# One-run float32r operands and a 29-column pitch for the low products of a binary 3x3 convolution

## The chip, the cores and the metric

The kernel runs on one core of one Trainium2 chip. The metric is the device time of one execution in microseconds. The engines named below are TensorE (PE in the profile, with its weight loads as PEld), VectorE (DVE), ScalarE (ACT), GpSimd (POOL) and SyncE (SP, which issues DMAs).

## The reference, cut to what matters

Four layers follow each other on 16 images of 256 channels of 28 x 28. The change is in layer 1, whose first part is a 3x3 convolution of signs with clipped float32 weights:

```python
residual = prelu(x, a_alpha1)
z = hardsign(x + _pc(a_move))
bw = jnp.clip(a_w, -1.0, 1.0)
y = conv_general_dilated(z, bw, (1, 1), ((1, 1), (1, 1)))
y = prelu(bn(y, a_bn1), a_alpha2)
...
u = einsum('bchw,oc->bohw', z2, bw2)
```

z holds only signs (hardsign's value is sign(x)), so the products are sums of weights with signs. Layers 0 and 2 are other binary convolutions, and layer 3 is attention over the 784 positions.

## The kernel before

Everything is in one function, `forward`, with helpers inside it. It is emitted twice: once as used here (`careful` is false), and once as a fallback that runs only if a flag asks for it, and doesn't run here.

In layer 1 the convolution uses a transformation along the image's height that makes two output rows out of four sums. For each image b, `transform` (VectorE) forms four combinations u = 0..3 of the padded sign rows, each 14 rows (HR) of 30 columns (S + 2) for two halves k of the channels. It writes them in bfloat16 to `vs16`, in which columns 0 and 29 of each row are zero, being combinations of the pads. `widen` (ScalarE, and VectorE for one at the start) copies each to `vs` in float32r, in the same layout. `move_on` copies `vs16` by DMA to `one_on`, shifted by one element, so that the middle tap of the bfloat16 products starts at an even column.

The weights are split in two. w1[0] holds float16 high parts and w1[1] float32r low parts. One sum, for an image b, a half mo of the output channels and a unit u, is 12 products of 128x128 weights with 14 x 28 = 392 (HN) columns: part 0, the six high products (k = 0, 1 and taps c = 0, 1, 2, on `vs16`, with `one_on` for the tap c = 1 from image 1 on), then part 1, the six low products on `vs`. All accumulate into one bank of PSUM, which has 512 columns, and are written as one run of 392. There are 16 x 2 x 4 = 128 such sums, so 768 high and 768 low products, all recorded at line 782.

Two sums share a tile `cv` of two banks. Units 1 and 2 make a pair: `sum_pair_a` (line 813, ScalarE) takes one bank into a temporary t, `sum_pair_b` (line 823, VectorE) adds and subtracts the other bank to and from it, into `uvs`. Units 0 and 3 make the other pair: `rows_out` (line 834, VectorE) adds each of its banks to `uvs` and writes the even and odd rows of y. `conv_pairs` issues both high parts of a pair first and then both low parts, `conv_pair` one whole sum, and `conv_alone`, used for the last image, gives a sum its own tile.

`iteration(b)` writes the order of PE, ACT, DVE and SP out by hand. While TensorE convolves image b, the other engines prepare image b + 1 (`enter` at line 732, `sign1` at line 738, `residual_a` and `residual_b`, `transform`, `widen`) and finish images b - 1 and b - 2 (`prelu_y`, the gates with their small products at lines 685 and 877, `branch1`, the 1x1 convolution `conv1x1` at line 909 with float32r operands read as one run of 392, `unit_u`, `unit_b`, `branch2`, `squares2`). `last_iteration` does the same for image 15. GpSimd's queue in these stages holds stores to memory (n0d at line 660, x2d at line 937), a few memsets and, between layer 0 and layer 1, four operations of `mom.doubt` for the flag that is used in layer 3.

Other lines that are spoken of: 376 are the products of `sign_layer` in layers 0 and 2, which read float16 signs in 14 rows of 28 from pads with a pitch of 30. In layer 0 all three taps come from the pads; later the middle tap comes from a copy shifted by one element. Line 392 is their first eviction on ScalarE. Line 478 (`keep_busy`) are idle products of 512 columns that bridge stretches where TensorE has nothing to do.

Of the kernel before, what the change touches and what calls it, by code (L numbers as in the profile page):

```python
# [27 lines left out]
F32 = mybir.dt.float32  # L28
FR = mybir.dt.float32r
F16 = mybir.dt.float16  # L30
BF16 = mybir.dt.bfloat16
I16 = mybir.dt.int16
I32 = mybir.dt.int32
AF = mybir.ActivationFunctionType
ALU = mybir.AluOpType
# [4 lines left out]
P = 128  # L40
B = 16
S = 28
N = S * S
HN = N // 2
HR = S // 2
# [31 lines left out]
def conv_seq_kernel(tc: tile.TileContext, d: dict, out: bass.AP):  # L77
    again = forward(tc, d, out, False)
    with tc.If(again > 0):
        forward(tc, d, out, True)  # L80
# [3 lines left out]
def forward(ctx: ExitStack, tc: tile.TileContext, d: dict, out: bass.AP, careful: bool):  # L84
# [3 lines left out]
    nc = tc.nc  # L88
    V, A, T = nc.vector, nc.scalar, nc.tensor
# [40 lines left out]
    def vtile(name):  # L130
        return const.tile([P, 2], F32, name=name)
# [334 lines left out]
    with tc.tile_pool(name="ps_conv", bufs=3, space=PSUM) as psc, \  # L466
            tc.tile_pool(name="ps_sm", bufs=2, space=PSUM) as pss:

        def conv_ps():
            return psc.tile([P, 2, 512], F32, tag="cv", name="cv")  # L470
# [9 lines left out]
        with tc.tile_pool(name="ph1", bufs=1) as ph:  # L480
# [21 lines left out]
            def temp(tag):  # L502
                return ph.tile([P, HN if careful else N], F32, tag=tag, name=tag, bufs=2)
# [83 lines left out]
            c1, c2, c3, c4 = (c_bn[:, i, :] for i in range(4))  # L587
            cc, zb2 = vtile("cc"), vtile("zb2")
            ra1, ra2, rf2, us1, ns1 = (vtile(q) for q in ("ra1", "ra2", "rf2", "us1", "ns1"))
# [7 lines left out]
            moved, b3c = vtile("moved"), vtile("b3c")  # L597
# [92 lines left out]
                    rows = slice(32 * g, 32 * g + 32)  # L690
                    tt(b_1[rows], h, b_1[rows], ALU.add)

            vs = ph.tile([P, 2, 4, 2, HR, S + 2], FR, tag="vs", name="vs")
            vs16 = vs if careful else ph.tile([P, 2, 4, 2, HR, S + 2], BF16, name="vs16")
            one_on = None if careful else ph.tile([P, 4, 2, HR, S + 2], BF16, name="one_on")

            def room_sums():
# [23 lines left out]
            def full(tag, name, bufs):  # L721
                return ph.tile([P, N], F32, tag=tag, name=name, bufs=bufs)
# [35 lines left out]
            def widen(b, u, copy=A.copy):  # L758

                if not careful:  # L760
                    v, w = (
                        t[:, b % 2, u].rearrange("p k i c -> p (k i c)") for t in (vs, vs16)
                    )
                    copy(v, w)  # L764

            rx = {}

# [5 lines left out]
                x = xs[b][:, k, :]  # L773
                V.scalar_tensor_tensor(x, rx.pop(k), ra1[:, k:k + 1], x, ALU.mult, ALU.add)

            def conv(b, mo, u, ps, parts=range(2)):

                for part in parts:
                    w, v = w1[part], (vs16, vs)[part]
                    moved = part == 0 and b > 0 and not careful  # L780
                    for k, c in [(k, c) for cs in (((0, 2), (1,)) if moved else ((0, 1, 2),)) for k in range(2) for c in cs]:
                        T.matmul(  # L782
                            ps.rearrange("p (a b) -> p a b", b=S),
                            lhsT=w[:, k, c, u, mo * P:(mo + 1) * P],
                            rhs=one_on[:, u, k, :, 0:S] if moved and c == 1 else v[:, b % 2, u, k, :, c:c + S],
                            start=((part, k, c) == (0, 0, 0)),
                            stop=((part, k, c) == (1, 1, 2)),
                        )


            uvs = wpool.tile([P, 2, 2, HN], F32, tag="wa", name="uvs")
            ys, us = {}, {}
            pairs = {}

            def conv_pair(b, mo, i, u, parts=range(2)):
                if i == 0 and 0 in parts:
                    pairs[b, mo, u > 0 and u < 3] = conv_ps()
                conv(b, mo, u, pairs[b, mo, u > 0 and u < 3][:, i, :HN], parts)

            def conv_alone(b, mo, i, u, parts=range(2)):  # L800
                if 0 in parts:
                    alone[i] = conv_ps()
                conv(b, mo, u, alone[i][:, i, :HN], parts)

            def conv_pairs(b, mo, *us):

                for part in range(2):
                    for i, u in enumerate(us):
                        conv_pair(b, mo, i, u, (part,))

            def sum_pair_a(b, mo):
                t = temp("t1")[:, :HN]
                A.activation(
                    t, pairs[b, mo, True][:, 0, :HN], AF.Identity, bias=c1[:, mo:mo + 1], scale=us1[:, mo:mo + 1]
                )
                pairs[b, mo] = t

            def sum_pair_b(b, mo):

                ps, t = pairs.pop((b, mo, True)), pairs.pop((b, mo))  # L820
                uv = uvs[:, mo]
                for i, s in enumerate((us1, ns1)):
                    V.scalar_tensor_tensor(uv[:, i], ps[:, 1, :HN], s[:, mo:mo + 1], t, ALU.mult, ALU.add)
                pairs[b, mo] = uv

            alone = {}

            def rows_out(b, mo, rows=range(2)):
                ps, uv = alone[rows[0]] if alone else pairs[b, mo, False], pairs[b, mo]
                if 0 in rows:  # L830
                    ys[b, mo] = full("yu", f"y{b}_{mo}", 6)
                two = ys[b, mo].rearrange("p (a two b) -> p two a b", two=2, b=S)
                for i in rows:
                    V.scalar_tensor_tensor(
                        two[:, i], ps[:, i, :HN].rearrange("p (a b) -> p a b", b=S), us1[:, mo:mo + 1],
                        uv[:, i].rearrange("p (a b) -> p a b", b=S), ALU.mult, ALU.add,
                    )

# [113 lines left out]
            def iteration(b):  # L952
# [15 lines left out]
                if two:  # L968
                    unit_b(b - 2, 0)
                    unit_b(b - 2, 1)  # L970
                sum_pair_a(b, 0)
                conv_pair(b, 0, 0, 0)
                h = hidden_a(b, hidden_x(b)) if one else None
                residual_a(b + 1, 0)
                sign1(b + 1, 1)
                sum_pair_b(b, 0)
                if one:
                    h = hidden_b(b, h)
                residual_a(b + 1, 1)
                residual_b(b + 1, 0)  # L980
                transform(b + 1, 1)
                residual_b(b + 1, 1)
                conv_pair(b, 0, 1, 3)
                rows_out(b, 0)
                if one:
                    g = gates(h)
# [3 lines left out]
                if one:  # L990
                    for k in range(2):
                        branch1_a(b - 1, k, g[:, 0])
                widen(b + 1, 1)
                conv_pairs(b, 1, 1, 2)
                for u in (1, 2):
# [9 lines left out]
                if two:  # L1005
                    branch2(b - 2, 0, g[:, 1])
                sum_pair_a(b, 1)
                sum_pair_b(b, 1)
                if one:
                    branch1_c(b - 1, 1)  # L1010
                widen(b + 1, 2)
                if two:
                    branch2(b - 2, 1, g[:, 1])
# [5 lines left out]
                for u in (0, 3):  # L1019
                    transform(b + 1, u)  # L1020
                    widen(b + 1, u)
# [3 lines left out]
                for s in aside[b + 1]:  # L1025
                    s.load()
                rows_out(b, 1)
                for late in lates:
                    late()
# [3 lines left out]
            def last_iteration(b):  # L1033
# [6 lines left out]
                for k in range(2):  # L1040
                    unit_b(b - 2, k)
                sum_pair_a(b, 0)
                h = hidden_b(b, hidden_a(b, hidden_x(b)))
                conv_pair(b, 0, 0, 0)
                sum_pair_b(b, 0)
                g = gates(h)
                for k in range(2):
# [3 lines left out]
                for k in range(2):  # L1051
                    branch1_b(b - 1, k)
                    branch1_c(b - 1, k)
                conv_pair(b, 1, 0, 1)
                rows_out(b, 0)
                squares2(b - 2, 0)
                branch2(b - 2, 1, g[:, 1])
# [7 lines left out]
                squares2(b - 2, 1)  # L1065
                px = hidden_x(B, TWO)
                conv_alone(b, 1, 0, 0, (0,))
                h = hidden_a(B, px, TWO)
                sum_pair_b(b, 1)
                h = hidden_b(B, h, TWO)  # L1070
                conv_alone(b, 1, 0, 0, (1,))
                rows_out(b, 1, (0,))
                g = gates(h, some=TWO)
                conv_alone(b, 1, 1, 3)
                branch2(b - 1, 0, g[:, 1])
                squares2(b - 1, 0)
# [13 lines left out]
            with tc.manual_schedule(engines={ET.PE, ET.DVE, ET.Activation, ET.SP}):  # L1090
# [23 lines left out]
                b = B - 1  # L1114
# [794 lines left out]
```

## Time and profile before

| | |
|---|---|
| time, median of 3 runs | 951.56 us (951.31 to 951.74) |
| profiled execution | 951.89 us |
| its span | 950.0 us |
| busy share PE, DVE, ACT, POOL | 98%, 80%, 71%, 14% |
| layer 1, its convolution | from 113.5 to 444.4 us |
| products at line 782, busy | 768 low 170.4 us, 768 high 168.6 us |
| granted TensorE clock, mean | 0.996 |

A line of a group names the code line, the engine and operation, out<-in by the program's names, for a product the weights' rows*columns and the moving operand's partitions x columns and type, and the count; then busy time and the mean duration of one, and the idle time of the engine before them with what ended it. Products overlap in the array, so a product's duration is longer than its share of the engine's time; the distance between the starts of two products is that share. The chain of waits is followed back from the last instruction to what released each, and is then shown in order of time: start, length, engine and line, number of instructions. A float32r operand is shown as f32 when a product reads it.

### The profile page before, as it was taken

To read this page: it belongs to the slowest core of one execution; us is meant where nothing else is said; L and a number is where in the kernel's file an instruction comes from. 1 tells how busy PE (TensorE), PEld (TensorE's weight loads), DVE (VectorE), ACT (ScalarE), POOL (GpSimd) and SP (SyncE) were. 2 spreads that over 40 slices of the span, in tenths; PEclk is the share of its full clock that TensorE was granted. 3 is DMA by queue.
4 is the path that set the end of the run, shared out by engine and by line. 5 is a ranking of instruction groups with operands and counts; after the bars stand their busy time and mean duration, and the time that the engine had idled before them with its cause. 6 is when DMAs were issued, how large, how long until landed. Compare 5 with 4: busy or idle time off the path is not lost.

```text
span 950.0 us, 14937 instructions
## 1 busy us (share of the span) xinstructions
PE 932.5 (98%) x5608; PEld 581.7 (61%) x5608; DVE 758.2 (80%) x1436; ACT 672.5 (71%) x1165; POOL 136.4 (14%) x145
## 2 busy tenths in 40 slices
PE   8999999999999999999999999999999999999995
PEld 4555678887888888787555555555444444444442
DVE  4777798999998899987788878889657767686865
ACT  6665568888887888865777757774867666666652
POOL 2001100000000000000000000000244343535340
PEclk9999999999999999999999999999999999999998
DMA  9877434445533444411655201111232524344212
GB/s 347 315 275 267 160 121 139 174 177 200 187 139 138 156 161 160 162 71 68 228 206 211 113 20 62 77 78 59 35 68 69 132 72 103 102 91 114 68 69 106
DMA packets 39334, 130.71 MB, mean 138 GB/s; under 512 B 4866, under 2 KB 16324, under 8 KB 39252
## 3 DMA queue, kind: packets, MB, share of 16 engines
q1 hardware_dynamic: 33332, 98.31, 28.9%
q0 software_dynamic: 5632, 30.54, 11.8%
q8 instruction: 46, 0.75, 0.3%
q10 hardware_dynamic: 288, 0.80, 0.2%
q14 instruction: 36, 0.29, 0.1%
HBM read 72.67 MB, written 32.11 MB: 110 GB/s over the span
## 4 chain that ended last, share of the span: by engine, by line
PE 95%; DVE 1%; ACT 1%; DMA 1%; SPq 1%; issue 0%; DVEq 0%; ACTq 0%
PE cv L376 30%; PE cv L782 29%; PE sc L1475 8%; PE av L1496 8%; PE cv L909 5%; PE mi L1452 5%; PE sm L1538 2%; PE unused L478 2%; PE mi L1556 2%; PE sm L1496 1%; DMA xs<-in_x_dram 1%; PE gate L877 1%; PE hid L685 1%; SPq L269 0%; DVE r L1522 0%
## 5 line engine op out<-in xcount | busy, mean ns | idle before, releaser
L782 PE MATMUL cv<-vs,w 128*128 128x392 f32 (+1 forms) x1296 | 272.4, 352 | 0.3 <-DVE vs L134 0.3
L376 PE MATMUL cv<-fpads,wpk 128*128 128x392 f16 (+1 forms) x1434 | 247.6, 329 | 1.7 <-DVE wpk L301 1.3
L376 PEld LDWEIGHTS <-wpk 128*128 128x128 f16 x1746 | 169.0, 97 | 124.4 <-DVE wpk L301 2.1
L782 PEld LDWEIGHTS cv<-vs,w 128*128 128x128 f32 x768 | 143.2, 190 | 6.3
L1479 ACT ACTIVATE es<-sc 128x784 f32<-128x784 f32 x112 | 87.3, 822 | 41.7 <-PE sc L1475 41.7
L782 PEld LDWEIGHTS <-w 128*128 128x128 f16 x768 | 69.4, 99 | 51.9 <-issue 9.1
L1475 PE MATMUL sc<-q,keyswa 64*128 64x392 f32 x448 | 89.9, 513 | 0.9 <-ACT es L1479 0.9
L1496 PE MATMUL av<-es,v 128*64 128x392 f32 x448 | 80.7, 499 | 0.0
L1239 DVE SCALAR_TENSOR_TENSOR p<-ab,vec 128x392 f32<-128x392 int16 x128 | 77.3, 617 | 0.0
L392 ACT ACTIVATE ab<-cv 128x392 int16<-128x392 f32 x64 | 31.8, 496 | 57.4 <-PE cv L376 54.5
L1489 POOL TENSOR_TENSOR sum<-sum,es 128x784 f32<-128x784 f32 x32 | 67.2, 2100 | 3.1 <-ACT es L1479 0.6
L1475 PEld LDWEIGHTS sc<-q,keyswa 64*128 64x128 f32 x448 | 38.9, 186 | 44.0 <-issue 17.1
L376 PE MATMUL cv<-shifted,wpk 128*128 128x392 f16 x312 | 60.2, 328 | 0.0
L782 PE MATMUL cv<-one_on,w 128*128 128x392 bf16 x240 | 59.4, 329 | 0.0
L1463 DVE COPY keyswa<-mi 64x392 f32<-64x392 f32 x31 | 16.3, 565 | 53.4 <-ACT q L1459 53.4
L1496 PEld LDWEIGHTS av<-es,v 128*64 128x64 f32 x448 | 29.4, 136 | 47.4 <-issue 47.0
L937 POOL DMA_DIRECT2D x2d<-x x16 | 8.6, 537 | 345.3 <-DVE x L931 284.9
L394 DVE SCALAR_TENSOR_TENSOR ab<-ab,cv 128x392 int16<-128x392 int16 x64 | 35.7, 558 | 27.7 <-ACT ab L392 27.5
L764 ACT CAST vs<-vs 128x840 fp32r<-128x840 bf16 x63 | 54.1, 882 | 2.5 <-DVE vs L134 2.5
L909 PE MATMUL cv<-z,fw 128*128 128x392 f32 x256 | 48.9, 342 | 0.1
L909 PEld LDWEIGHTS cv<-z,fw 128*128 128x128 f32 x256 | 46.1, 188 | 0.9 <-ACT z L901 0.9
L1452 PE MATMUL mi<-p,wqk 128*128 128x392 f32 x124 | 45.1, 505 | 0.1
(313 smaller groups left out, 1529.0 us busy)
## 6 DMA issues: line engine op xcount, KB each, us to landing
xs<-in_x_dram SPq DMA_DIRECT2D x30, 784.0 KB, 5.1
one_on<-vs SPq DMA_DIRECT2D x60, 209.8 KB, 2.7
x2d<-x POOLq DMA_DIRECT2D x16, 784.0 KB, 3.6
out_dram<-p SPq DMA_DIRECT2D x15, 784.0 KB, 3.8
shifted<-fpads SPq DMA_DIRECT2D x26, 449.8 KB, 2.7
p<-x2d POOLq DMA_DIRECT2D x14, 784.0 KB, 6.9
p<-x2d SPq DMA_DIRECT2D x13, 784.0 KB, 5.9
n0d<-n POOLq DMA_DIRECT2D x16, 392.0 KB, 4.4
```

Source lines behind the costliest of these rows:

```text
L376: T.matmul(pss[j][:, n // size if careful else h, :rows * S].rearrange("p (a b) -> p a b", b=S), lhsT=w[:, n, c, :], rhs=src[:, blocks[j][ ...
L392: A.activation(by_halves(ab[:, 1], blocks[j]), ps, AF.Copy, scale=1.0 / PACK)
L394: V.scalar_tensor_tensor(a, b, -PACK, ps, ALU.mult, ALU.add)
L764: copy(v, w)
L782: T.matmul(ps.rearrange("p (a b) -> p a b", b=S), lhsT=w[:, k, c, u, mo * P:(mo + 1) * P], rhs=one_on[:, u, k, :, 0:S] if moved and c == 1 ...
L909: T.matmul(ps[:, h, :HN], lhsT=w[:, k, mo * P:(mo + 1) * P], rhs=z2[b][:, k, h * HN:(h + 1) * HN], start=(k + i == 0), stop=(k + i == 2),)
L1239: V.scalar_tensor_tensor(p, y, alpha[:, mo:mo + 1], y, ALU.mult, ALU.max, accum_out=mom.sums[:, 0, at // 2:at // 2 + 1] if mom.by_sums(at, ...
L1452: T.matmul(ps[:, h, :HN], lhsT=wqk[:, k, :], rhs=x[b][:, k, h * HN:(h + 1) * HN], start=(k == 0), stop=(k == 1))
L1475: T.matmul(ps[:, h, :HN], lhsT=chunk[rows], rhs=qs[b][rows], start=True, stop=True)
L1479: A.activation(e, ps[:, :, :HN], AF.Exp, scale=0.125)
L1489: (V if late else nc.gpsimd).tensor_tensor(sums[b, late], sums[b, late], e, ALU.add)
L1496: T.matmul(ps[64 * h:64 * h + 64, :HN], lhsT=w, rhs=e[:, h, :], start=start, stop=stop)
```

## The change

The float32r tile `vs` drops one of the two zero columns: its rows are 29 apart instead of 30, so that the zero at the end of a row is the zero at the start of the next. A tap c of a low product then is the run of LONG = 14 x 29 = 406 elements that starts at c; each 29th column of the result is of no use. Two zeros are added behind the last row, by one memset on GpSimd. The sums in PSUM get the same pitch of 29: the low products write runs of 406, the high ones write 28 of every 29 columns, except for the first of each sum, which writes all 29 (reading 29 columns of each row), so that the 29th columns hold a number. `sum_pair_a`, `sum_pair_b` and `rows_out` read 28 of 29 through `of_rows`. `widen` copies 29 of 30 columns of each row. `vs16`, `one_on` and the weights stay as they are.

```diff
-            vs = ph.tile([P, 2, 4, 2, HR, S + 2], FR, tag="vs", name="vs")
-            vs16 = vs if careful else ph.tile([P, 2, 4, 2, HR, S + 2], BF16, name="vs16")
+            LONG = HR * (S + 1)
+            if careful:
+                vs = vs16 = ph.tile([P, 2, 4, 2, HR, S + 2], FR, tag="vs", name="vs")
+            else:
+                vs16 = ph.tile([P, 2, 4, 2, HR, S + 2], BF16, name="vs16")
+
+                vs = ph.tile([P, 2, 4, 2, LONG + 2], FR, tag="vs", name="vs")
+                nc.gpsimd.memset(vs[:, :, :, :, LONG:].bitcast(F32), 0.0)
+
+            def of_rows(ps, i, whole=False):
+
+                if careful:
+                    return ps[:, i, :HN].rearrange("p (a b) -> p a b", b=S)
+                return ps[:, i, :LONG].rearrange("p (a b) -> p a b", b=S + 1)[:, :, 0:S + whole]
...
             def widen(b, u, copy=A.copy):
 
                 if not careful:
-                    v, w = (
-                        t[:, b % 2, u].rearrange("p k i c -> p (k i c)") for t in (vs, vs16)
-                    )
-                    copy(v, w)
+                    v = vs[:, b % 2, u, :, 0:LONG].rearrange("p k (i c) -> p k i c", c=S + 1)
+                    copy(v, vs16[:, b % 2, u, :, :, 0:S + 1])
...
-            def conv(b, mo, u, ps, parts=range(2)):
+            def conv(b, mo, u, i, ps, parts=range(2)):
 
                 for part in parts:
                     w, v = w1[part], (vs16, vs)[part]
+                    long = part == 1 and not careful
                     moved = part == 0 and b > 0 and not careful
                     for k, c in [(k, c) for cs in (((0, 2), (1,)) if moved else ((0, 1, 2),)) for k in range(2) for c in cs]:
+                        if long:
+                            rhs = v[:, b % 2, u, k, c:c + LONG]
+                        elif not careful and (part, k, c) == (0, 0, 0):
+                            rhs = v[:, b % 2, u, k, :, 0:S + 1]
+                        else:
+                            rhs = one_on[:, u, k, :, 0:S] if moved and c == 1 else v[:, b % 2, u, k, :, c:c + S]
                         T.matmul(
-                            ps.rearrange("p (a b) -> p a b", b=S),
-                            lhsT=w[:, k, c, u, mo * P:(mo + 1) * P],
-                            rhs=one_on[:, u, k, :, 0:S] if moved and c == 1 else v[:, b % 2, u, k, :, c:c + S],
+                            ps[:, i, :LONG] if long else of_rows(ps, i, (part, k, c) == (0, 0, 0)),
+                            lhsT=w[:, k, c, u, mo * P:(mo + 1) * P], rhs=rhs,
                             start=((part, k, c) == (0, 0, 0)),
                             stop=((part, k, c) == (1, 1, 2)),
                         )
...
                 A.activation(
-                    t, pairs[b, mo, True][:, 0, :HN], AF.Identity, bias=c1[:, mo:mo + 1], scale=us1[:, mo:mo + 1]
+                    t.rearrange("p (a b) -> p a b", b=S), of_rows(pairs[b, mo, True], 0), AF.Identity,
+                    bias=c1[:, mo:mo + 1], scale=us1[:, mo:mo + 1],
                 )
...
-                uv = uvs[:, mo]
+                uv, ps1 = uvs[:, mo], of_rows(ps, 1)
                 for i, s in enumerate((us1, ns1)):
-                    V.scalar_tensor_tensor(uv[:, i], ps[:, 1, :HN], s[:, mo:mo + 1], t, ALU.mult, ALU.add)
+                    V.scalar_tensor_tensor(
+                        uv[:, i].rearrange("p (a b) -> p a b", b=S), ps1,
+                        s[:, mo:mo + 1], t.rearrange("p (a b) -> p a b", b=S), ALU.mult, ALU.add,
+                    )
...
                     V.scalar_tensor_tensor(
-                        two[:, i], ps[:, i, :HN].rearrange("p (a b) -> p a b", b=S), us1[:, mo:mo + 1],
+                        two[:, i], of_rows(ps, i), us1[:, mo:mo + 1],
                         uv[:, i].rearrange("p (a b) -> p a b", b=S), ALU.mult, ALU.add,
                     )
```

More of the change, by code (lines that the diff above doesn't have):

```diff
@@ L797, in conv_pair @@
                     pairs[b, mo, u > 0 and u < 3] = conv_ps()
-                conv(b, mo, u, pairs[b, mo, u > 0 and u < 3][:, i, :HN], parts)
+                conv(b, mo, u, i, pairs[b, mo, u > 0 and u < 3], parts)
             def conv_alone(b, mo, i, u, parts=range(2)):
@@ L802, in conv_alone @@
                     alone[i] = conv_ps()
-                conv(b, mo, u, alone[i][:, i, :HN], parts)
+                conv(b, mo, u, i, alone[i], parts)
             def conv_pairs(b, mo, *us):
```

## The prediction

> **What bounds the kernel now.** I read the chain of waits first, in order of time, because it says which engine's work is never waited out by another. From 114 us to 444 us, all of layer 1's 3x3 convolution, it is TensorE without a break. One image's pieces (start us, us, what):
>
> ```profile
> 235.75 6.43 PE cv L782 x36
> 242.19 0.32 PE hid L685 x4
> 242.51 2.25 PE cv L782 x12
> 244.76 0.34 PE gate L877 x4
> 245.10 8.56 PE cv L782 x48
> 253.66 2.88 PE cv L909 x16
> ```
>
> They add to 20.8 us per image, 96 of the 112 large products being the convolution's. The table by stages says whether another engine is near; the columns are window: us, then busy us of PE, weight loads, DVE, ACT, POOL, then the granted clock, the DMA share and GB/s:
>
> ```profile
> 235.00:256.00 21.00, 21.00 (x123) 17.17 (x122) 19.11 (x40) 18.54 (x30) 0.53 (x1) 1.00 0.50 182
> ```
>
> PE is busy all 21.0 us at full clock, DVE 19.1, ACT 18.5. So a nanosecond on a product of line 782 is a nanosecond on the end, and DVE and ACT have about 1.9 and 2.5 us per image in which to lose some. The groups by shape then give the two kinds of product (busy us, mean ns of one):
>
> ```profile
> L782 PE MATMUL cv<-vs,w 128*128 128x392 f32 x768 | 170.4, 367 | 0.0
> L782 PE MATMUL cv<-vs,w 128*128 128x392 bf16 x528 | 109.2, 330 | 0.3 <-DVE vs L134 0.3
> L782 PE MATMUL cv<-one_on,w 128*128 128x392 bf16 x240 | 59.4, 329 | 0.0
> L909 PE MATMUL cv<-z,fw 128*128 128x392 f32 x256 | 48.9, 342 | 0.1
> ```
>
> These durations overlap, since a product starts before the last one's results are out. What counts is the distance between starts, which the timeline of PE gives:
>
> ```profile
> 249.90 0.49 PE L782 MATMUL cv<-one_on,w 128*128 128x392 bf16 x2
> 250.24 0.83 PE L782 MATMUL cv<-vs,w 128*128 128x392 bf16 x4
> 250.90 0.49 PE L782 MATMUL cv<-one_on,w 128*128 128x392 bf16 x2
> 251.09 2.57 PE L782 MATMUL cv<-vs,w 128*128 128x392 f32 x12
> ```
>
> High products: 250.24 to 250.90 for four, 165 ns each. Low products: the two one_on products from 250.90 take 0.33, so the twelve low ones start in truth at 251.23, and the conv1x1 product after them starts at 253.50 by the same view: 2.27 / 12 = 189 ns; I use 189.5 (the x36 and x48 pieces, less their high half at 165.9, give 191 to 192 with the switches between kinds). The conv1x1 of line 909 has the same 128x128 float32 weight load and the same 392 columns, but reads them as one run: 2.88 / 16 = 180 ns (179.8). Rows therefore cost the low products 9.7 ns each, and that is what the change goes after.
>
> **The change, part by part.**
>
> *Low products, 768 of them.* Afterwards each reads one run, but of 406 columns. The price of a column: the 512-column products of line 478 lie on the chain as 6.47 us for 30, 215.7 ns; the fp16 products of line 376 as 38.99 us for 235, 165.9 ns for 392; (215.7 - 165.9) / 120 = 0.415 ns. Fourteen columns are 5.8 ns, so 179.8 + 5.8 = 185.6 ns, a gain of 3.9 each, 768 x 3.9 = 3.0 us. More than half of the rows' 9.7 ns goes to the added columns. Bounds: if the 180 ns of line 909 are set by the weight load (188 ns records, one per product) and not by the columns, 406 also cost 179.8 and the gain is 9.7 x 768 = 7.4 us; if the rows are not what costs, they take 189.5 + 5.8 = 195.3, a loss of 4.5 us. I take 185.6: clean column price, nearest row.
>
> *The first high product of each sum, 128 of them* (16 images x 2 halves of channels x 4 units), widens from 392 to 406 columns so that the 29th ones are written too: 128 x 5.8 = 0.74 us lost.
>
> *The other 640 high products* still have 392 columns, but write rows of 28 with a pitch of 29 into PSUM, where all large products of this trace write one run. This is the open price. Below: nothing, if the writing side takes any address; a gain is excluded, since 392 columns at 0.415 are already all of their 165 ns but 3. Above, the nearest row is a reader's: line 376 in layer 0 reads all three taps from the pads, so every third product's 14 rows begin one 2-byte element off, and its chain piece is 35.18 us for 207, 170.0 ns against the 165.9 of the later stage where a shifted copy serves that tap. Three times 4.1 is 12.2 ns for 14 rows on an odd element, 0.87 a row. With pitch 29, every second output row starts on an odd element: 7 x 0.87 = 6.1 ns if the writer pays as the reader does, 640 x 6.1 = 3.9 us. If all 14 rows pay, 12.2 ns, 7.8 us. I take 6.1, as odd starts are what that row shows paying, and even starts (taps 0 and 2 there) pay next to nothing. The break-even is (3.0 - 0.74) / 640 = 3.5 ns per product.
>
> [...]
>
> *The reads of PSUM with pitch 29* (ACT line 813, DVE lines 823 and 834). Line 834 already uses rows (618 ns), line 823 one run (616 to 622): rows as such cost nothing on DVE. ACT's 662 ns may grow; nothing shows it. Even 10% on all of them is 2 x 4 x 0.06 = 0.5 us per image, spread over the two engines and covered by their 1.9 and 2.5 us. Uncovered it would be 0.5 x 16 = 8 us, but PE would have to run into their results, and the waits view has no product of layer 1 waiting longer than 0.3 us.
>
> *Widening* copies 812 instead of 840 elements: 63 ACT casts of 881 ns, at 0.83 ns an element ((822 - 496) / 392, line 392) 23 ns less each; nothing for the end, as PE does not wait for them. The one DVE cast at 114.72 (597 ns) may fall to DVE's slower rate of 1.05 ns ((1030 - 618) / 392), 0.3 us more; it would end at 115.6, and unit 2's low products come six products after 115.81. Cover 1.3 us; without it 0.3 us.
>
> *The POOL memset* stands behind the last n0d store (108.56 us, waiting for DVE) and ahead of four operations for doubts that nobody needs before layer 3. A 128x1 memset there took 0.10 us; this one of 32 elements may take 0.3. It adds a wait of PE for POOL; behind it are all products of layer 1, but the first that reads the zeros starts at 115.81, six us later. No DMA is added or moved; move_on still copies from the bf16 tile.
>
> **Sum.** -3.0 + 0.74 + 3.9 = +1.6 us. The profiled execution took 951.89 (span 950.0 and 1.9 around it) and would become 953.5; the median shown is 0.33 lower, so 953.2. That is +0.17%, inside the 0.2% that a measurement can tell from no change.
>
> **Rivals.**
>
> 1. *Pitched writes are free.* For: high products here read rows of 28 with a pitch of 30 at 165 ns, next to the bare column price. Against: odd rows on the reading side are not free. -3.0 + 0.74 = -2.3: 949.3.
> 2. *Every row of a pitched write pays*, the mechanism that ends slower: TensorE's write of 14 separate rows, at 12.2 ns on each of 640 products. It decides from about 6.5 ns on, where the sum reaches +1.9 us. For: float32 rows at even and odd starts alike cost the low products about 10 ns on the reading side, and sums are float32. Against: 2-byte rows at even starts pay nothing. -3.0 + 0.74 + 7.8 = +5.5: 957.1.
> 3. *The low products gain nothing* (the rows are not their cost; the change then doesn't do what it is said to): 195.3 ns each, +4.5 + 0.74 + 0 to 3.9: 956.8 to 960.7. Against: line 909, alike in all but the rows.
> 4. *Weight loads set the 180 ns*: -7.4 + 0.74 + 0 to 3.9: 944.9 to 948.8. For: each float32 load is recorded with 188 ns. Against: the loads of line 877, before products of 2 columns, follow each other faster than that (four products in 0.34 us on the chain).
>
> **Chances.** Forecast 0.36, rivals 0.30, 0.22, 0.06, 0.06. Faster by over 0.2% (under 949.7): most of rival 1 (0.24) and rival 4, 0.30. Within: the rest of rival 1 and two thirds of the forecast, 0.06 + 0.24 = 0.30. Slower (over 953.5): the forecast's upper third 0.12, rivals 2 and 3, 0.40. The range runs from 948.6, below rival 1, to 958.5, above rival 2: it leaves out rival 4, most of rival 3 and the tails of 1 and 2, under 0.2. The forecast's own range, from a write price of 4 to 8 ns, is 951.9 to 954.4.
>
> **What would show it.** Low group, now 128x406: mean 367 down by about 4, and the distance between starts near 185.6; 180 speaks for rival 4, 195 for rival 3. High group of 392 columns: mean 330 up by 6; unchanged is rival 1, up by 12 rival 2. The first high product: up by 6, or, if pitch costs, less than the others. The chain must still be TensorE throughout; if ACT or DVE appear in it between 120 and 440 us, the covered costs were not covered. An x48 piece (24 low, 4 first and 20 other high products) would go from 8.56 to 8.61 us by the forecast (-0.094 + 0.023 + 0.122), to 8.49 by rival 1, to 8.73 by rival 2.

## The result and the profile after

The changed kernel takes 953.86 us (median of 15 runs, 952.38 to 955.29), the kernel before, on the same chip, 951.9. The ratio is 1.002 with a 95% interval of 1.0013 to 1.0027: slower by about 1.9 us, on the edge of what was to be called no change. The forecast was +1.6 us. The profiled execution took 954.27 us, its span is 952.2.

The chain of waits after, in order of time, answers the pieces shown of before (start us, us, what; the products moved from line 782 to 799):

```profile
236.34 6.50 PE cv L799 x36
242.84 0.32 PE hid L685 x4
243.17 2.26 PE cv L799 x12
245.43 0.34 PE gate L897 x4
245.77 8.61 PE cv L799 x48
254.38 2.87 PE cv L929 x16
```

It is still TensorE throughout, and each piece with convolution products is a little longer: x36 6.43 to 6.50, x48 8.56 to 8.61 as forecast. The sharpest measure is the time per image, from the start of one 1x1 convolution to that twelve images later. Before (line 909) and after (line 929):

```profile
170.50 2.88 PE cv L909 x16
...
419.98 2.88 PE cv L909 x16
```

```profile
170.75 2.87 PE cv L929 x16
...
421.63 2.87 PE cv L929 x16
```

That is 249.48 / 12 = 20.790 us before and 250.88 / 12 = 20.907 after: 0.117 us an image, 1.9 us for 16, all of the loss. The groups by shape after (busy us, mean ns) show its parts:

```profile
L799 PE MATMUL cv<-vs,w 128*128 128x406 f32 x768 | 167.9, 363 | 0.0
L799 PE MATMUL cv<-vs,w 128*128 128x392 bf16 x400 | 89.8, 337 | 0.3 <-DVE vs L134 0.3
L799 PE MATMUL cv<-one_on,w 128*128 128x392 bf16 x240 | 61.1, 338 | 0.0
L799 PE MATMUL cv<-vs,w 128*128 128x406 bf16 x128 | 44.4, 347 | 0.0
```

The low products got shorter although they have 14 columns more (367 to 363). The high ones of 392 columns, whose operands did not change, got longer (330 and 329 to 337 and 338); what changed for them is the write into rows with a pitch of 29, and the experiments test that. The 128 first ones are the longest of the high ones. The other engines' work is as it was: the three readers of pitched sums take 667, 622 and 616, and 618 ns, as before (666, 622 and 616, 618), and the casts 860 instead of 882.

### The profile page after: what moved, and what is told of

It reads as the page before. It is cut to its first block, busy times and chain, and to the rows that moved or that the text cites. A ratio compares the mean times of both kernels' runs of the same rounds, so it can differ in the third digit from the quotient of the medians.

```text
span 952.2 us, 14947 instructions
## 1 busy us (share of the span) xinstructions
PE 933.3 (98%) x5602; PEld 581.3 (61%) x5608; DVE 758.3 (80%) x1436; ACT 671.6 (71%) x1165; POOL 136.3 (14%) x146
## 4 chain that ended last, share of the span: by engine, by line
PE 95%; ACT 1%; DMA 1%; DVE 1%; SPq 1%; issue 0%; DVEq 0%; ACTq 0%
PE cv L376 30%; PE cv L799 29%; PE sc L1495 9%; PE av L1516 8%; PE cv L929 5%; PE mi L1472 5%; PE sm L1558 2%; PE unused L478 2%; PE mi L1576 2%; PE sm L1516 1%; DMA xs<-in_x_dram 1%; PE gate L897 1%; PE hid L685 1%; ACT es L1499 0%; SPq L269 0%
## 5 line engine op out<-in xcount | busy, mean ns | idle before, releaser
L799 PE MATMUL cv<-vs,w 128*128 128x406 f32 (+2 forms) x1296 | 273.7, 353 | 0.3 <-DVE vs L134 0.3
L774 ACT CAST vs<-vs 128x812 fp32r<-128x812 bf16 x63 | 52.6, 860 | 2.4 <-DVE vs L134 2.4
```

Source lines behind the costliest of these rows:

```text
L774: copy(v, vs16[:, b % 2, u, :, :, 0:S + 1])
L799: T.matmul(ps[:, i, :LONG] if long else of_rows(ps, i, (part, k, c) == (0, 0, 0)), lhsT=w[:, k, c, u, mo * P:(mo + 1) * P], rhs=rhs, start ...
```

## Experiments

Two theories of the pitched write were to be told apart. Theory 1: a row of PSUM that starts on an odd element costs TensorE extra, an even one nothing. Theory 2 (the forecast's rival 2): every separate row costs. All images' times below are worked out as above, over the same twelve images.

**One run for the high products.** The edit to the changed kernel, in `conv`:

```diff
-    ps[:, i, :LONG] if long else of_rows(ps, i, (part, k, c) == (0, 0, 0)),
+    ps[:, i, :LONG] if long else of_rows(ps, i, True) if not careful and (part, k, c) == (0, 0, 0)
+    else of_rows(ps, i) if careful else img(ps[:, i, 0:0 + HN]),
```

> The changed kernel, but with 640 high products (all but the first of each sum) writing their 392 columns as one run, as in the kernel before; the low products still read and write runs of 406. High and low sums then do not lie on the same columns, so the output is not the reference's: it is a kernel for its time only. Theory 1 (rows written from an odd start pay) and theory 2 (every row of a pitched write pays) agree: the distance between the starts of those high products returns from 171.5 to 165 ns, 4.0 us of the changed kernel's 953.9 go, and what is left is the low products' gain less the widened first ones: 949.5 to 950.3. If the price lay elsewhere (evictions reading with a pitch, widening, the memset), the time stays near 953.9.

Measured: 951.48 us beside 952.26 of the kernel before, a ratio of 0.9992 (0.9983 to 1.0001). Behind another high product, these products return to the 165 ns from start to start that they had before. The chain of this kernel:

```profile
170.47 2.87 PE cv L930 x16
...
419.15 2.87 PE cv L930 x16
```

20.723 us an image, 0.184 below the changed kernel. Forty such products an image: the write with pitch 29 costs 4.6 ns each. What the change wins without it, 0.067 us an image or 1.1 us in all, is less than the 1.6 to 2.4 expected; the first high products explain most of that (below).

**Pitch 30, even and odd.** In both, the first high product writes 420 columns, so that every later write lies on written columns, and the others write 28 of 30 from column 0, or from column 1:

```diff
+    def rows30(ps, i, at, n):
+        return ps[:, i, :HR * 30].rearrange("p (a b) -> p a b", b=30)[:, :, at:at + n]
...
-    rhs = v[:, b % 2, u, k, :, 0:S + 1]
+    rhs = v[:, b % 2, u, k]
...
-    ps[:, i, :LONG] if long else of_rows(ps, i, (part, k, c) == (0, 0, 0)),
+    ps[:, i, :LONG] if long else of_rows(ps, i) if careful
+    else rows30(ps, i, 0, S + 2) if (part, k, c) == (0, 0, 0) else rows30(ps, i, 0, S),
```

> The changed kernel, but with the 640 high products writing rows of 28 with a pitch of 30, so that every row starts on an even element, and the first high product of each sum writing all 30 columns of each row (420). High and low sums do not lie on the same columns, so the output is not the reference's. Theory 1 (odd starts pay): high products at 165 to 166 ns apart, time as with one run plus 0.7 us for the wider first product: 950.3 to 951.0. Theory 2 (every row pays): 171.5 ns, 954 to 955.

> As the kernel with a pitch of 30, but each of the 640 high products' rows starts one element later, so that all 14 rows start on an odd element. The output is not the reference's. Theory 1: twice the price of pitch 29, which has 7 such rows: 165 + 12.5 = 177 to 178 ns apart, 958 to 959.5. Theory 2: 171.5 ns, 954 to 955.

Measured: 951.36 (0.9991, 0.9982 to 1.0) for even rows and 957.55 (1.0055, 1.0041 to 1.0069) for odd ones. The chains and one group of each, even first:

```profile
170.73 2.87 PE cv L933 x16
...
419.41 2.87 PE cv L933 x16
```

```profile
L802 PE MATMUL cv<-one_on,w 128*128 128x392 bf16 x240 | 59.5, 329 | 0.0
```

```profile
171.85 2.87 PE cv L933 x16
...
425.65 2.87 PE cv L933 x16
```

```profile
L802 PE MATMUL cv<-one_on,w 128*128 128x392 bf16 x240 | 62.6, 344 | 0.0
```

Even: 248.68 / 12 = 20.723 us, the same as one run. Odd: 253.80 / 12 = 21.150 us, 0.427 more, 10.7 ns for each of the 40 products. The two programs differ only in the column on which the rows start. Seven odd rows cost 4.6 ns, fourteen 10.7, fourteen even ones nothing: theory 1 holds and theory 2 falls. Fourteen odd rows were expected to cost 12.5 ns; the mean is less, for a reason given below. All rows have 28 columns, so one that starts on an odd column also ends just before one (columns 1 to 28, the next is 29), and the runs can't say which of the two ends is paid for. That the first product's 420 columns cost no more than its 406 in rows of 29 (20.723 us both) is taken up below.

**One run from column 1.** As the first experiment, with `ps[:, i, 1:1 + HN]`.

> The changed kernel, but with the 640 high products writing one run of 392 that starts on column 1. The output is not the reference's. Theory 1, in its form that an odd row costs one access more: one access of 0.9 ns per product, so 166 ns apart, 0.6 us above the run that starts on column 0, about 950.5. If instead every pair of an odd run were split, the products would take far more than 171.5 ns and the time would pass 960. Theory 2: no price, as the run starting on column 0.

Measured: 951.08 us (0.9986, 0.9976 to 0.9995); 248.44 / 12 = 20.703 us an image, no more than the run from column 0, where 0.6 us more in all were expected. The groups, column 0 first, show why the time can't tell: the high products are some 1 to 2 ns longer, as one odd start a product would make them, and the low ones 1 ns shorter.

```profile
L799 PE MATMUL cv<-vs,w 128*128 128x406 f32 x768 | 167.8, 363 | 0.0
L799 PE MATMUL cv<-one_on,w 128*128 128x392 bf16 x240 | 59.5, 329 | 0.0
```

```profile
L799 PE MATMUL cv<-vs,w 128*128 128x406 f32 x768 | 167.2, 362 | 0.0
L799 PE MATMUL cv<-one_on,w 128*128 128x392 bf16 x240 | 59.8, 331 | 0.0
```

Why the low ones are shorter was not tried. An odd start was paid per row and not per pair of elements: 196 shifted pairs cost 1 to 2 ns a product, fourteen odd rows 10.7.

**Pitch 30 alone.** The kernel before, with all sums, and their readers, on rows of 28 with a pitch of 30:

```diff
+    PITCH, AT = (S, 0) if careful else (30, 0)
+    def of_rows(ps, i):
+        return ps[:, i, AT:AT + HR * PITCH].rearrange("p (a b) -> p a b", b=PITCH)[:, :, 0:S]
...
-    ps.rearrange("p (a b) -> p a b", b=S),
+    of_rows(ps, i),
```

> The kernel before, with one change: all sums of layer 1's 3x3 convolution lie in PSUM with a pitch of 30 instead of 28; the low products still read rows, and every reader reads 28 of 30. The output is the reference's. Theory 1 (only rows written from an odd start pay, and readers do not mind a pitch): no change, 951.5 to 952.7, high products 165 ns and low products 189 to 190 ns apart. Theory 2 (every row of a pitched write pays): 768 high products and perhaps the low ones at 4 to 6 ns, 955 to 961.

Measured: 952.89 us (1.0003, 0.9993 to 1.0012), and 249.48 / 12 = 20.790 us an image, the kernel before's to the digit. A pitch of 30 costs TensorE nothing that shows (its groups keep their 367, 330 and 329 ns), and `rows_out` keeps its 618 ns; the other two readers never come onto the chain of these images.

**Low products in one run of 392, and of 336.** These ask what the rows cost on the reading side, and whether columns or weight loads set the distance (the forecast's rivals 3 and 4). The edit to the kernel before, with 336 in place of 392 for the second:

```diff
-    ps.rearrange("p (a b) -> p a b", b=S),
+    ps[:, :392] if part == 1 and not careful else ps.rearrange("p (a b) -> p a b", b=S),
...
-    rhs=one_on[:, u, k, :, 0:S] if moved and c == 1 else v[:, b % 2, u, k, :, c:c + S],
+    rhs=v[:, b % 2, u, k].rearrange("p a b -> p (a b)")[:, c:c + 392] if part == 1 and not careful
+    else one_on[:, u, k, :, 0:S] if moved and c == 1 else v[:, b % 2, u, k, :, c:c + S],
```

> The kernel before, but each low product reads one run of 392 elements of its tile instead of 14 rows of 28, and writes 392 columns as before; it reads wrong elements, so the output is not the reference's and only the time counts. If the rows are the low products' price, they come to 180 ns apart as the products of the 1x1 convolution, 9.6 x 768 = 7.4 us less: 944.5 to 945.5. If they stay at 185 to 186, as in the changed kernel with 406 columns, the columns cost nothing and something else sets that distance: 948.5 to 949.5.

> As the kernel with low runs of 392, but of 336 columns (12 rows' worth), so that part of the sums is left out; the output is not the reference's. If columns set the distance (0.415 ns each), the low products come to 157 ns, or to the high ones' neighbourhood, and the time falls by another 17 to 18 us to 927 to 929, unless DVE or ACT then bound the image. If the float32 weight load (188 ns recorded, one per product) sets it, the distance stays at 180 ns and the time at that of the run of 392.

Measured: 946.55 us (0.9943, 0.9927 to 0.9959) and 942.68 (0.9899, 0.9883 to 0.9915), beside 952.53 of the kernel before. PE's timeline, 392 first, with the last two high products, the twelve low ones and the conv1x1 behind them:

```profile
249.61 0.50 PE L782 MATMUL cv<-one_on,w 128*128 128x392 bf16 x2
249.81 2.46 PE L782 MATMUL cv<-vs,w 128*128 128x392 f32 x12
252.10 1.24 PE L910 MATMUL cv<-z,fw 128*128 128x392 f32 x6
```

```profile
247.82 0.50 PE L782 MATMUL cv<-one_on,w 128*128 128x392 bf16 x2
248.01 2.17 PE L782 MATMUL cv<-vs,w 128*128 128x336 f32 x12
250.03 1.24 PE L910 MATMUL cv<-z,fw 128*128 128x392 f32 x6
```

The two high products take 0.33 us, so the low ones start at 249.94 and 248.15. (252.10 - 249.94) / 12 = 180.0 ns, and (250.03 - 248.15) / 12 = 156.7: the rows cost 9.5 ns of 189.5, and 56 columns cost 23.3 ns, 0.416 each, with the same float32 weight load in front (188 and 189 ns recorded). The distances came as the columns said; the times did not fall as far (944.5 to 945.5 and 927 to 929 had been expected). With low runs of 336 the chain passes to the other engines, and PE waits before its high products, in the last figures of this group:

```profile
L782 PE MATMUL cv<-vs,w 128*128 128x392 bf16 x528 | 109.1, 330 | 9.1 <-DVE y L835 8.1 <-DVE sf L328 0.7 <-DVE vs L134 0.3
```

Its convolution products run from 113.6 to 433.7 us, 20.0 us for each of the 16 images, and between 150 and 400 us PE is busy 239.4 of 250. That mean hides a nearer bound in the early images, which the chain of the run of 392 shows:

```profile
149.62 2.87 PE cv L910 x16
...
182.74 1.15 DVE y L835 x2
...
203.44 1.15 DVE y L835 x2
...
273.09 2.87 PE cv L910 x16
...
415.43 2.87 PE cv L910 x16
```

From 162 to 262 us that chain runs over ACT and DVE alone and comes round every 20.70 us (203.44 - 182.74); from 273 us on it is TensorE, at 142.34 / 7 = 20.33 us an image. So in those early images TensorE stops being the bound 0.09 us below the 20.79 of the kernel before, and only in the later ones near 20 us. Neither ACT nor DVE is busy throughout (219.3 and 231.5 of 250 us with runs of 336), so it is likely their waits for each other, in the order written by hand, that set the 20.70; no run had another order.

**The first product's price.** To the first experiment, one more edit: the first high product reads one run of 406, and writes the same 406 columns as before, put as one run.

```diff
-    rhs = v[:, b % 2, u, k, :, 0:S + 1]
+    rhs = v[:, b % 2, u, k].rearrange("p a b -> p (a b)")[:, 0:LONG]
...
-    ps[:, i, :LONG] if long else of_rows(ps, i, True) if not careful and (part, k, c) == (0, 0, 0)
+    ps[:, i, :LONG] if long or not careful and (part, k, c) == (0, 0, 0)
```

> The kernel whose other high products write one run of 392 (its output is not the reference's), with one more edit: the first high product of each sum reads its 406 columns as one run of the bfloat16 tile instead of 14 rows of 29, so it reads wrong elements. In that kernel the first product's start lies 177 ns ahead of the next one's within a pair's second sum, which is what 420 columns take, and a product of 420 columns took the same. If a row of 29 two-byte elements is read as 30, the one run takes 171 ns and an image 20.68 us instead of 20.72 (8 x 6 ns). If the price belongs to the first product of a sum in another way (its 406 written columns, the start of a group), it stays at 177 ns and 20.72 us.

Measured once each: 950.41 us beside 953.64 of the kernel before; (418.75 - 170.71) / 12 = 20.670 us an image and 171 ns, where rows of 29 had 177. The 420 columns of the pitch-30 kernels also take 177. So a row of 29 two-byte elements was read here in the time of one of 30.

**A version that beats both.** By the runs, a low product costs 24 ns more than a high one (189.5 to 165): 9.5 for its rows, and the rest also in one run (180). Rounding the low parts of the weights to float16 lets them read the bfloat16 signs as the high ones do:

```diff
-    w1 = [ph.tile([P, 2, 3, 4, 256], dt, name=f"w1_{i}") for i, dt in enumerate((HI, FR))]
+    w1 = [ph.tile([P, 2, 3, 4, 256], dt, name=f"w1_{i}") for i, dt in enumerate((HI, FR if careful else F16))]
...
-    vs = ph.tile([P, 2, 4, 2, HR, S + 2], FR, tag="vs", name="vs")
-    vs16 = vs if careful else ph.tile([P, 2, 4, 2, HR, S + 2], BF16, name="vs16")
+    vs = vs16 = ph.tile([P, 2, 4, 2, HR, S + 2], FR if careful else BF16, tag="vs", name="vs")
...
-    moved = part == 0 and b > 0 and not careful
+    moved = b > 0 and not careful
...
-    stop=((part, k, c) == (1, 1, 2)),
+    stop=((part, k, c) == (1, 1, 1 if moved else 2)),
```

`widen` does nothing then. The sums differ from the kernel before's in the rounding of the low parts.

> A version meant to beat both: the kernel before with the low parts of the weights rounded to float16 instead of float32r, so that the low products read the bfloat16 signs (and the shifted copy for the middle tap) as the high ones do, and the widened tile and its 64 casts fall away. What changes in the computation is the rounding of the low parts. By the distances, each low product goes from 189 to 165 ns: 24 x 768 = 18.4 us less, 933.5. An image would take PE 19.65 us, and DVE's 19.1 busy us would be close behind: if DVE's waits appear on the chain, up to 938.

Measured: 934.62 us, ratio 0.9813 (0.9798 to 0.9829). Its chain:

```profile
206.87 2.87 PE cv L904 x16
209.74 6.01 PE cv L777 x36
...
226.52 2.88 PE cv L904 x16
```

19.65 us an image, and TensorE from 170 us to the end of the convolution at 427 us (between 154 and 170 us the chain runs over ACT and DVE). Without the casts ACT is busy 188.2 us between 150 and 400, where the kernel before has 215.0, and the chain stays with PE below the 20 us at which low runs of 336 lost it. The casts stood on that lost chain (7.9% of it from 225 to 265 us); that taking them away is what moved the bound is the likely reading, and no run takes away the casts alone.

## Why the prediction was right, step by step

The forecast said +1.6 us with the pitched write paying on odd rows, and +1.9 came, by that mechanism. But its three terms were each off, by +24, +50 and -60 ns an image, and the errors mostly cancelled: that the sum came so close is luck, that the mechanism held is not. The stated range, 948.6 to 958.5, would have held a faster kernel too.

| per image, ns | forecast | measured | how |
|---|---|---|---|
| 48 low products | -187 | -163 | not measured alone: -67 of the first experiment, less the +96 of the next line |
| 8 first products | +46 | +96 | 165 to 177 ns; half of it confirmed by the run of 406 |
| 40 other high products | +244 | +184 | changed kernel less first experiment |
| sum | +103 | +117 | |

*Low products.* The forecast took 185.6 ns from the row of line 909 and the bare price of a column; the table's -163 / 48 = -3.4 gives 186.1. Right, and its two bounds are refuted: 392 columns take 180.0 and 336 take 156.7, so neither weight loads (rival 4) nor a price that ignores rows (rival 3) set the distance.

*First products.* Sized at half their price: 0.74 us forecast, 8 x 12 ns x 16 = 1.5 measured. The step priced 29 columns a row as 29, and the chip read them in the time of 30 (177 ns, as 420 columns). This is most of why the first experiment stayed above its expectation.

*Pitched writes.* The mechanism was taken from the reading side, 0.87 ns for each row that starts on an odd element (170.0 against 165.9 ns at line 376), and the writing side did the same thing: 10.7 / 14 = 0.76 a row when all are odd, 4.6 / 7 = 0.66 when every second is. The forecast's 6.1 ns was 1.5 too much. In the trace the later products of a sum pay 6.5 (165 to 171.5), and the second and third, which were 167 and 169 apart before, only 2 to 3. With all rows odd, the later ones pay 12.5 (165 to 177.5) and the second and third about 8. So the later products pay 0.9 a row in both kernels, about the reading side's price, and the forecast went wrong in taking all forty to pay it. It looks as if part of the price lay beside a delay that the second and third had anyway; what that delay is was not tried, and stays open.

What the runs show of separate rows is this: rows of 28 with a pitch of 30 cost 0.000 us an image (20.723, as in one run), the same rows one column further 0.427, and a run of 392 from column 1, whose pairs of columns are all shifted, 1 or 2 ns a product at most. So it seems to be the broken pairs at the ends of rows that pay; that reading is inferred from these three runs, and none shows a pair by itself.

*Costs put at nothing.* The reads of PSUM kept their durations, as the groups showed, and the wait for POOL never shows: the memset ran at 4.28 us and not behind the last n0d store, where the prediction had put it. The strided DVE cast did not lose its rate either (0.58 us, 0.60 before). But the cover that the prediction gave the readers, 1.9 and 2.5 us an image, was read from the engines' busy time and is not there in the early images: in the run of 392, whose ACT and DVE work is the kernel before's, their own chain comes round in 20.70 us, against TensorE's 20.79, and all three readers stand on it. The term came out at nothing because the readers kept their durations, and not because it was covered.

```profile
4.28 0.37 POOL L700 MEMSET vs<- 128x32 f32 x1
```

## What to carry to other kernels

Here rows were best counted in pairs of elements on both sides of TensorE: a 2-byte operand row that begins on an odd element cost 0.87 ns, a PSUM row that begins on an odd column 0.66 to 0.9, the odd row length of 29 another 0.43 a row (177 to 171 for 14), and even rows written with a pitch of 30 nothing (20.723 us an image, as in one run). By these figures a pitch is to be chosen even before it is chosen small. Where a layout helps one operand, price the same layout at every other product that shares the sum: here 40 + 8 high products paid for 48 low ones. (That holds for the 2-byte rows; the rows of float32r cost 9.5 ns for 14, and no run separates their odd starts from their even ones.) And when a bound engine is relieved, ask at once how far the next bound is, and in which images: here it was 0.09 us away in the early ones and 0.8 in the later ones (20.8 to 20.0), and with the casts gone TensorE ran at 19.65.

## What the runs showed that was not expected

- A row of 29 bfloat16 elements was read in the time of 30 (177 ns for 14 rows, 171 for a run of 406).
- A run of 392 columns from an odd column of PSUM costs 1 or 2 ns at most and nothing in the time of an image (20.703 against 20.723 us), though 14 odd rows cost 10.7 ns.
- Low runs of 336 columns saved 16 x 48 x 32.8 ns = 25 us of TensorE's work (189.5 to 156.7), and only 9.9 us of time: TensorE spent most of the rest in waits for the other engines.
- In the early images ACT and DVE, though neither is busy throughout, go round in 20.70 us, 0.09 us less than TensorE's 20.79.
